# Four-layer network on one core: softmax reciprocals turned by DMA and set into PSUM by ScalarE, 5x5 convolutions that add to the shared sum in place, and a smaller pace

## The chip, the cores and the metric

The kernel runs on one core of one Trainium2 chip. The metric is the device time of one launch in microseconds (us). The engines of the core are TensorE (PE in the profile, its weight loads PEld), VectorE (DVE), ScalarE (ACT), GpSimd (POOL) and SyncE (SP), which here only issues DMAs. Each works through its own queue in order.

## The reference

Four images of 128 channels and 64 x 64 pixels pass through four residual layers. Each layer is `x = x + layer(groupnorm(x))` in float32.

```python
# layer 0: full attention over the 4096 pixels of an image, one head of 128
scores = einsum('bic,bjc->bij', q, k) * c ** -0.5
attn = softmax(scores, axis=-1)
out = einsum('bij,bjc->bic', attn, v)
# layer 1: a 5x5 convolution, its kernel built from radial weights
c = build_kernel(weightsxx, weightsidentity, XhatXhat, identity, indsxx, indsidentity)
x = conv(pad(x, 2), c)
# layer 2: two selective scans (one direction each), 64 channels, 64 states
dA = exp(delta[..., None] * A);  dBx = (delta * xt)[..., None] * Bm[:, :, None, :]
h = associative_scan(a1*a2, a2*b1 + b2)      # along the 4096 pixels
y = einsum('bldn,bln->bld', h, Cm) + D * xt
# layer 3: a 3x3 convolution (its offsets are zero) and a bias
```

## The kernel before

**Two streams of work.** The scans of layer 2 are cut into ticks: `scan_core` runs over 4 images x 4 chunks of 1024 pixels x 2 directions x 16 groups of states x 2 halves of channels, 1024 ticks in all, 256 to an image. A tick multiplies the drive on POOL (line 1268), takes the decay's exponential on ScalarE (1261), runs the recurrence on VectorE (`tensor_tensor_scan`, 1278), and multiplies by C on VectorE (1281) or, in a fixed share of the ticks, on POOL (1299). TensorE sums states into `y` (1317) every few ticks. Everything else (attention, convolutions, the scans' operands, the way back to the output) is a chain of Python generators, `images()`, whose `yield` values say how much TensorE work was just written.

**The order is written by hand.** `manual_schedule` leaves the order of instructions as the program writes it. Between the two halves of a tick the loop draws from `images()` until a credit is used up:

```python
PRODUCT, HOP, SLOT, PACE, ENDPACE, AHEAD = 0.86, 1.7, 0.7, 2.8, 1.5, 4
credit = min(credit + pace / 2, pace)
while credit > 0:
    credit -= next(work, pace)
```

So `PACE` sets how much of an image is written beside one tick; in the last image's scan it is `ENDPACE`. `before(b)` is called four ticks (`AHEAD`) before image b's scan begins: where that image's first operands are not written yet, it draws `images()` without a limit until they are. Image 0 has no scan beside it until its operands exist.

**Attention** goes over 8 blocks of 512 queries, each with 32 steps of 128 keys. Step u writes the scores of u (`sc`, line 487), their exponential on ScalarE into a ring of 8 slots in the tile `exchange` (493), and the product with the values of step u - 2 into the PSUM bank `acc` (499). The sums of the exponentials come in two ways. In image 0 (`fill` set) VectorE and POOL add every other step's tile into `sided` and `sidep` (541). In images 1 to 3, four matmuls of 32 columns, one in each group of 32 PSUM partitions, add four steps at a time into the bank `zp` (521). When a block is done (two steps into the next), ScalarE copies the sums (`zs`, 547) and `acc` (`raw`, 552) to SBUF. Then `turn` (564) takes the sums through TensorE into columns, `invert` (573, 575) takes reciprocals on VectorE, `widen_out` (479) spreads them over partitions through TensorE, and `settle` (587, 588) multiplies and adds on VectorE; these stand 1, 2, 4 and 5 steps after, and use the bank `z`, which the next block's `zp` uses too. `turn` and `widen_out` each count one `PRODUCT`.

**The 5x5 convolution** (`conv_pairs`) makes two output rows at a time and goes over 4 chunks of 1024 pixels. In images 1 to 3 (`lean`) a chunk has three sums of products (969): one that both rows share (`pq`, 10 products) and one for each row (`pe`, 15 each). ScalarE copies the shared sum to SBUF (`q`, 982), and one matmul with the identity (996) adds it to each row's bank. Image 0 goes another way (`wide`), with POOL adding `q` to the rows.

**Queues and buffers that matter.** All loads of the scan go out on SP: `br` and `cr` (1239), 512 KB each, once in two ticks, and `de` and `dx` (1233) at changes of chunk. The tiles tagged `w` in the pool `bg` have four buffers, `raw` and `zs` one, the scan's rows three.

Of the kernel before, what the change touches and what calls it, by code (L numbers as in the profile page):

```python
# [32 lines left out]
P = 128  # L33
# [12 lines left out]
PRODUCT, HOP, SLOT, PACE, ENDPACE, AHEAD = 0.86, 1.7, 0.7, 2.8, 1.5, 4  # L46
# [6 lines left out]
def conv_preact_kernel(  # L53
# [388 lines left out]
    def attention(b, xs, xn, v, st, safe, loads):  # L442
# [15 lines left out]
        def row_max(blk):  # L458
# [14 lines left out]
            mb[blk] = pools["bg"].tile([P, MM], F32, tag="w", bufs=4, name=f"mb_{b}_{blk}")  # L473
# [69 lines left out]
        def evict_sums(blk):  # L543
            zs = None
            if not fill:
                zs = pools["bg"].tile([P, MM], F32, tag="zs", bufs=1, name=f"zs_{b}_{blk}")
                nc.scalar.copy(zs, zp.pop(blk))
            state[blk] = None, zs

        def evict(blk):  # L550
            raw = pools["bg"].tile([P, MM], F32, tag="raw", bufs=1, name=f"raw_{b}_{blk}")
            nc.scalar.copy(raw, acc.pop(blk))  # L552
            state[blk] = raw, state[blk][1]
# [44 lines left out]
        for u in range(N):  # L598
# [11 lines left out]
            if w >= 0:  # L610
# [224 lines left out]
    def conv_pairs(b, xs, tag, st, st2, lean):  # L835
# [89 lines left out]
        steps, done = [], None  # L925
# [17 lines left out]
        for c in range(L // CH):  # L943
            j = c * CK
            if c < 2:
                piece(2 + c)
            if c < 3:
                differences(c + 1)
            accs = [
                (bank("s", f"pq_{b}_{c}"), ((SUM12, image, 2 * j + 2), (SUM34, image, 2 * j + 4))),  # L950
                (bank("a", f"pe0_{b}_{c}"),
                 ((0, image, 2 * j), (1, diff, j), (3, diff, j + 1))),
                (bank("z", f"pe1_{b}_{c}"),
                 ((0, image, 2 * j + 1), (2, diff, NP + j + 1), (4, diff, NP + j + 2))),
            ]
            if wide:
                total, first, last = (combo(n) for n in range(3))
                accs = [
                    (accs[0][0], (accs[0][1][1], (HSUM, total, j))),
                    (bank("y", f"pm_{b}_{c}"), ((HDIF, diff, j),)),  # L960
                    (accs[1][0], ((0, first, j), (3, diff, j + 1))),
                    (accs[2][0], ((2, last, j), (4, diff, NP + j + 2))),
                ]
            for n, (acc, parts) in enumerate(accs):
                k, total = 0, len(parts) * K5
                for w, view, r in parts:
                    for dx in range(K5):
                        k += 1
                        nc.tensor.matmul(  # L969
                            flat(acc), matrix(w, dx), view(r, dx),  # L970
                            start=k == 1, stop=k == total and (n == 0 or not lean),
                        )
                        if k == 3 and done is not None:
                            done()
                            done = None
                        if k % 3 == 0:
                            yield 3 * PRODUCT
                if n == 0:
                    qs = pools["bg"].tile([P, MM], F32, tag="w", bufs=4, name=f"q_{b}_{c}")

                    def done(acc=acc, qs=qs, c=c):
                        nc.scalar.copy(qs, acc)
                        for y in range(0 if lean else 2):
# [4 lines left out]
                elif wide and n == 1:  # L988
# [686 lines left out]
```

## Time and profile before

| | |
|---|---|
| median of 3 runs | 4425.56 us (4419.15 to 4431.18) |
| the profiled execution | 4426.94 us, of which the span is 4425.1 us |
| TensorE, VectorE, POOL, ScalarE busy | 88%, 84%, 81%, 54% of the span |
| image 0 alone, to the first tick's drive | 694.7 us |
| 1024 ticks, first to last drive | 694.7 to about 4361 us |
| DMA | 726 MB, mean 164 GB/s |

The profile cuts the span into 40 slices, each with the busy share of every engine in tenths. Groups of instructions carry the line, the engine, the tiles, the count, the busy time, the mean of one in nanoseconds, and the engine's idle time just before them with what ended it. A float32 product shows as two TensorE records[...]; the records overlap, and their ends are modelled, so distances between starts are used for TensorE.

### The profile page before, as it was taken

Reading aid. Unit: us, or ns where it says so; the run is one execution under the profiler, and the core shown is the slowest. Engines: PE = TensorE matmul, PEld = TensorE weight load, DVE = VectorE, ACT = ScalarE, POOL = GpSimd, SP = SyncE. Lnnn points to the kernel's source line nnn. Section 1 sums busy time; section 2 is a strip of 40 time slices with the busy share of each in tenths; the row PEclk is TensorE's granted clock in tenths of the full one; section 3 lists DMA queues with packets and bytes.
Section 4 is the critical chain, followed back from the end, with each engine's and each line's share of the span. In section 5 each row is a group of like instructions: output and inputs, shape, how many; then the busy total and the mean of one; then the engine's idle time right before and its main releaser. Section 6 shows DMA issues by size and latency. Waiting matters only on the chain. (4 is left out here: it accounts for less than half of the span.)

```text
span 4425.1 us, 42907 instructions
## 1 busy us (share of the span) xinstructions
PE 3896.3 (88%) x13352; PEld 1486.0 (34%) x13352; DVE 3702.6 (84%) x3471; ACT 2377.4 (54%) x4301; POOL 3603.6 (81%) x1713
## 2 busy tenths in 40 slices
PE   8999997999999979999989889999989657575667
PEld 4444433333333323333333333333333112121212
DVE  4722217999999989999999889999999899999996
ACT  3333217666665376666664576666643754444533
POOL 3433307999999968999989889999999789999995
PEclk9999999999999989999999989999999868787888
DMA  1000016545555565544545564555555666656562
GB/s 64 21 1 1 0 53 231 185 167 176 177 176 182 176 238 198 176 176 168 185 173 181 201 228 168 175 177 175 176 181 177 223 221 206 228 195 232 187 227 84
DMA packets 216302, 726.05 MB, mean 164 GB/s; under 512 B 26240, under 2 KB 27520, under 8 KB 215808
## 3 DMA queue, kind: packets, MB, share of 16 engines
q1 hardware_dynamic: 214144, 722.49, 47.1%
q8 instruction: 107, 1.75, 0.2%
q14 instruction: 131, 1.07, 0.1%
q10 hardware_dynamic: 1920, 0.73, 0.1%
HBM read 653.98 MB, written 69.14 MB: 163 GB/s over the span
## 5 line engine op out<-in xcount | busy, mean ns | idle before, releaser
L1268 POOL TENSOR_TENSOR db<-dx,br 128x1024 f32<-128x1024 f32 x1024 | 2399.5, 2366 | 224.8 <-DMA dx<-dxd 76.7
L1261 ACT ACTIVATE da<-de,a_neg 128x512 f32<-128x512 f32 (+1 forms) x1640 | 1303.1, 797 | 759.6 <-DVE da L1278 305.0
L487 PE MATMUL sc<-r,x 128*128 128x512 f32 x2048 | 1082.2, 611 | 22.5 <-ACT last L1294 9.7
L499 PE MATMUL acc<-exchange,v 128*128 128x512 f32 x2048 | 1048.6, 594 | 2.7 <-ACT raw L552 0.5
L1299 POOL TENSOR_TENSOR hc<-hc,cr 128x1024 f32<-128x1024 f32 x386 | 913.3, 2366 | 22.9 <-ACT last L1294 20.9
L1281 DVE TENSOR_TENSOR hc<-da,cr 128x512 f32<-128x512 f32 (+1 forms) x1003 | 839.5, 837 | 65.7 <-issue 1.3
L1278 DVE TENSOR_TENSOR_SCAN da<-da,last,db 128x512 f32<-128x512 f32 (+1 forms) x480 | 863.1, 1798 | 22.6 <-POOL db L1268 17.7
L493 ACT ACTIVATE exchange<-sc 128x512 f32<-128x512 f32 x1024 | 603.6, 589 | 503.1 <-PE sc L487 494.6
L1317 PE MATMUL y<-hc,sel 128*32 128x512 f32 x4096 | 604.8, 650 | 284.4 <-POOL hc L1299 230.9
L487 PEld LDWEIGHTS sc<-r,x 128*128 128x128 f32 x2048 | 361.8, 190 | 596.5 <-issue 376.7
L499 PEld LDWEIGHTS acc<-exchange,v 128*128 128x128 f32 x2048 | 386.9, 190 | 500.6 <-issue 478.5
L1278 DVE TENSOR_TENSOR_SCAN hc<-da,last,db 128x512 f32<-128x512 f32 (+1 forms) x288 | 490.9, 1705 | 6.4 <-ACT da L1261 3.3
L1278 DVE TENSOR_TENSOR_SCAN da<-da,da,db 128x512 f32<-128x512 f32 x365 | 469.7, 1287 | 6.8 <-ACT da L1261 6.6
L541 POOL TENSOR_TENSOR sidep<-sidep,exchange 128x512 f32<-128x512 f32 x120 | 170.8, 1423 | 273.4 <-ACT exchange L493 271.1
L1317 PEld LDWEIGHTS y<-hc,sel 128*32 128x32 f32 x4096 | 114.4, 113 | 715.5 <-POOL hc L1299 315.2
L1278 DVE TENSOR_TENSOR_SCAN hc<-da,hc,db 128x512 f32<-128x512 f32 x251 | 322.0, 1283 | 32.7 <-ACT da L1261 8.9
L541 DVE TENSOR_TENSOR sided<-sided,exchange 128x512 f32<-128x512 f32 x120 | 95.9, 799 | 221.7 <-ACT exchange L493 220.3
L1278 DVE TENSOR_TENSOR_SCAN da<-da,db 128x512 f32<-128x512 f32 (+1 forms) x158 | 232.4, 1471 | 13.1 <-ACT da L1261 10.1
L703 PE MATMUL pcm<-xpm,cs 128*128 128x512 f32 x432 | 214.5, 646 | 25.2 <-ACT xpm L392 25.2
L969 PE MATMUL pe<-df,exchange 128*128 128x512 f32 x480 | 214.2, 595 | 0.0
L521 PE MATMUL zp<-exchange,ones 128*32 128x512 f32 x1536 | 205.3, 601 | 9.6 <-DVE xs L588 9.5
L1294 ACT COPY last<-da 128x1 f32<-128x1 f32 x474 | 73.8, 156 | 259.7 <-DVE hc L1281 257.2
(239 smaller groups left out, 2838.8 us busy)
## 6 DMA issues: line engine op xcount, KB each, us to landing
br<-bm SPq DMA_DIRECT2D x512, 512.0 KB, 5.2
cr<-cm SPq DMA_DIRECT2D x512, 512.0 KB, 4.0
de<-dd SPq DMA_DIRECT2D x64, 512.0 KB, 4.9
dx<-dxd SPq DMA_DIRECT2D x64, 512.0 KB, 6.2
x<-in_x_dram SPq DMA_DIRECT2D x16, 512.0 KB, 6.0
xs<-in_x_dram SPq DMA_DIRECT2D x16, 512.0 KB, 6.6
xsd<-xs SPq DMA_DIRECT2D x16, 512.0 KB, 6.8
xcd<-xc SPq DMA_DIRECT2D x16, 512.0 KB, 2.9
```

The costliest lines, as they stand in the source:

```text
L487: nc.tensor.matmul(sc, xn[:, bass.ts(j, P)], rq[blk], start=True, stop=True)
L493: nc.scalar.activation(pt, sc, AF.Exp)
L499: nc.tensor.matmul(acc[blk], v[:, j, :], ring[:, u % NRING, :], start=j == 0, stop=j == NJT - 1)
L541: eng.tensor_tensor(s, s, ring[:, u % NRING, :], ALU.add)
L703: nc.tensor.matmul(acc.rearrange("p (r w) -> p r w", w=W), weights[:, t, :], xp[:, y : y + RPM, dx : dx + W], start=t == 0, stop=t == k * ...
L969: nc.tensor.matmul(flat(acc), matrix(w, dx), view(r, dx), start=k == 1, stop=k == total and (n == 0 or not lean),)
L1261: nc.scalar.activation(da, rep["de", b, c, d, g][:, bass.ts(h, size)], AF.Exp, scale=a_neg[:, at(i)])
L1268: nc.gpsimd.tensor_tensor(dbs[i], rep["dx", b, c, d, g], rows["b", b, c, d, q], ALU.mult)
L1278: nc.vector.tensor_tensor_scan(h, da, db[:, cut], before, ALU.mult, ALU.add)
L1281: nc.vector.tensor_tensor(hc[:, cut], h, rows["c", b, c, d, q][:, cut], ALU.mult)
L1299: nc.gpsimd.tensor_tensor(hcs[i], hcs[i], rows["c", b, c, d, q], ALU.mult)
L1317: nc.tensor.matmul(y[r : r + SG, :], sel, hcs[first + gg][:, bass.ts(h, MM)], start=False, stop=q == NQ - 1, tile_position=(0, r), skip_gr ...
```

## The change

*Attention.* `turn`, `invert` and `widen_out` stay only for the last block of an image. For the others, the block's sums, already in SBUF, are written to DRAM (`spill`), read back so that partition p holds the sums of queries 4p to 4p + 3 (`gather`), added and inverted on VectorE (`invert_rows`), written to DRAM (`put_rows`) and read back as one row to all partitions (`fetch_rows`). When the next block is done, ScalarE copies that tile into a PSUM bank (`stage_rows`), and `settle` follows a step later. In image 0 the two side tiles are first summed by two matmuls of 32 columns in `evict_sums`. `raw` moves to the `w` buffers, and `mb`, used only in a second pass for extreme inputs, takes its old one.

*Convolution, images 1 to 3.* ScalarE copies the shared sum of a chunk from its bank into the first row's bank; the first row's products are added there in place, and the second row's in the shared bank itself. The identity matmuls go. The order becomes: shared sum of chunk c, second row of chunk c - 1, first row of chunk c; the shared sums alternate between the banks `s` and `z`.

*Pace.* `PACE` goes from 2.8 to 2.75.

```diff
-PRODUCT, HOP, SLOT, PACE, ENDPACE, AHEAD = 0.86, 1.7, 0.7, 2.8, 1.5, 4
+PRODUCT, HOP, SLOT, PACE, ENDPACE, AHEAD = 0.86, 1.7, 0.7, 2.75, 1.5, 4
...
 def evict_sums(blk):
...
+            elif blk + 1 < NM:
+                zs = pools["bg"].tile([P, MM], F32, tag="zs", bufs=1, name=f"zs_{b}_{blk}")
+                pz = bank("z", f"pz_{b}_{blk}")
+                for g, e in enumerate("dp"):
+                    nc.tensor.matmul(
+                        pz[g * 32 : (g + 1) * 32, :], ones[:, :32], sides.pop((blk, e)),
+                        start=True, stop=True, tile_position=(0, g * 32), skip_group_check=True,
+                    )
+                nc.scalar.copy(zs[:64], pz[:64])
...
+        RUN = MM // P
+
+        def spill(blk):
+            raw, zs = state[blk]
+            n = 2 if fill else 4
+            zd = dram.tile([4, MM], F32, tag="zp", name=f"zd_{b}_{blk}")
+            nc.sync.dma_start(zd[:n], zs[0 : n * 32 : 32, :])
+            state[blk] = raw, zd[:n]
+
+        def gather(blk):
+            raw, zd = state[blk]
+            zt = small.tile([P, 4, RUN], F32, tag="zt", name=f"zt_{b}_{blk}")
+            n = zd.shape[0]
+            nc.sync.dma_start(zt[:, :n, :], zd.rearrange("g (p j) -> p g j", j=RUN))
+            state[blk] = raw, zt[:, :n, :]
+
+        def invert_rows(blk):
+            raw, zt = state[blk]
+            z = zall[:, b * NJT + blk * TPM : b * NJT + (blk + 1) * TPM]
+            nc.vector.tensor_reduce(z, zt.rearrange("p g j -> p j g"), AX.X, ALU.add)
+            zr = small.tile([P, RUN], F32, tag="zr", name=f"zr_{b}_{blk}")
+            nc.vector.reciprocal(zr, z)
+            state[blk] = raw, zr
+
+        def put_rows(blk):
+            raw, zr = state[blk]
+            zd = dram.tile([P, RUN], F32, tag="zd", name=f"zi_{b}_{blk}")
+            nc.sync.dma_start(zd, zr)
+            state[blk] = raw, zd
+
+        def fetch_rows(blk):
+            raw, zd = state[blk]
+            rb = pools["bg"].tile([P, MM], F32, tag="w", bufs=4, name=f"rb_{b}_{blk}")
+            row = zd.rearrange("p j -> (p j)").unsqueeze(0)
+            nc.sync.dma_start(rb, row.to_broadcast([P, MM]))
+            state[blk] = raw, rb
+
+        def stage_rows(blk, tag):
+            raw, rb = state[blk]
+            pb = bank(tag, f"rz_{b}_{blk}")
+            nc.scalar.copy(pb, rb)
+            state[blk] = raw, pb
...
                 if d == NJT - 1:
                     evict_sums(blk - 1)
                     evict(blk - 1)
-                    for n, f in ((1, turn), (2, invert), (4, widen_out), (5, settle)):
+                    for n, f in (
+                        (2, spill), (4, gather), (7, invert_rows), (9, put_rows), (11, fetch_rows)
+                    ):
                         after(u, n, f, blk - 1)
+                    if blk > 1:
+                        stage_rows(blk - 2, "z")
+                        after(u, 1, settle, blk - 2)
+                    cost += PRODUCT if fill else 0.0
             for f, args in later.pop(u, ()):
                 f(*args)
-                cost += PRODUCT if f in (turn, widen_out) else 0.0
...
         values(N - 4)
+        stage_rows(blk - 1, "s")
         yield PRODUCT
         while due:
             sums(due.pop(0)[0])
             yield PRODUCT
+        settle(blk - 1)
...
+        def shared_of(c):
+            j = c * CK
+            held[c] = bank("sz"[c % 2], f"pq_{b}_{c}")
+            yield from group(
+                held[c], ((SUM12, image, 2 * j + 2), (SUM34, image, 2 * j + 4))
+            )
+
+        def second_of(c):
+            nonlocal done
+            j, acc = c * CK, held.pop(c)
+            yield from group(
+                acc, ((0, image, 2 * j + 1), (2, diff, NP + j + 1), (4, diff, NP + j + 2)), True
+            )
+            done = lambda: add(c, 1, acc)
+
+        def first_of(c):
+            nonlocal done
+            j, acc = c * CK, owns.pop(c)
+            yield from group(
+                acc, ((0, image, 2 * j), (1, diff, j), (3, diff, j + 1)), True
+            )
+            done = lambda: add(c, 0, acc)
+
+        def part(c):
+            owns[c] = bank("a", f"pe0_{b}_{c}")
+            nc.scalar.copy(owns[c], held[c])
+
+        for c in range(NCK + 1 if lean else 0):
+            if c < NCK:
+                advance(c)
+                yield from shared_of(c)
+                done = lambda c=c: part(c)
+            if c > 0:
+                yield from second_of(c - 1)
+            else:
+                yield HOP
+                done()
+                done = None
+            if c < NCK:
+                yield from first_of(c)
...
-                    if lean:
-                        nc.tensor.matmul(acc, ident, qs, start=False, stop=True)
-                        yield PRODUCT
```

`group` writes the products of one sum (with its last argument true, without a fresh start of the bank), calls `done()` after the third product and yields three `PRODUCT` at a time; image 0's path goes through it too, unchanged in its products.

More of the change, by code (lines that the diff above doesn't have):

```diff
@@ L472, in row_max @@
             spread(pb, m)
-            mb[blk] = pools["bg"].tile([P, MM], F32, tag="w", bufs=4, name=f"mb_{b}_{blk}")
+            mb[blk] = pools["bg"].tile([P, MM], F32, tag="raw", bufs=1, name=f"mb_{b}_{blk}")
             nc.scalar.copy(mb[blk], pb)
@@ L550, in evict @@
+        def fetch_rows(blk):
[9 more added lines that the diff above has]
+            state[blk] = raw, pb
         def evict(blk):
-            raw = pools["bg"].tile([P, MM], F32, tag="raw", bufs=1, name=f"raw_{b}_{blk}")
+            raw = pools["bg"].tile([P, MM], F32, tag="w", bufs=4, name=f"raw_{b}_{blk}")
@@ L924, in conv_pairs @@
         K5 = 5
-        steps, done = [], None
+        done = None
         taps5 = more[0] if wide else exchange(b)[:, : NTAP * C].rearrange("p (k c) -> p k c", c=C)
@@ L941, in add, with advance @@
             st2.squares(i, chunk(xs, c, y), xs[:, 0:1])
-        for c in range(L // CH):
-            j = c * CK
+        def advance(c):
             if c < 2:
@@ L948, in conv_pairs @@
                 differences(c + 1)
-            accs = [
[L950 to L954, printed above, removed]
-            ]
[L956 to L963, printed above, removed]
@@ L964, in conv_pairs, with group @@
-            for n, (acc, parts) in enumerate(accs):
[L965 to L977, printed above, removed]
+        def group(acc, parts, begun=False):
+            nonlocal done
+            k, of_all = 0, len(parts) * K5
+            for w, view, r in parts:
+                for dx in range(K5):
+                    k += 1
+                    nc.tensor.matmul(
+                        flat(acc), matrix(w, dx), view(r, dx),
+                        start=k == 1 and not begun, stop=k == of_all, skip_group_check=lean,
+                    )
+                    if k == 3 and done is not None:
+                        done()
+                        done = None
+                    if k % 3 == 0:
+                        yield 3 * PRODUCT
@@ new lines, in conv_pairs @@
+        NCK, held, owns = L // CH, {}, {}
+        def shared_of(c):
[11 more added lines that the diff above has]
+            done = lambda: add(c, 1, acc)
@@ new lines, in first_of @@
+        def first_of(c):
+            nonlocal done
+            j, acc = c * CK, owns.pop(c)
+            yield from group(
+                acc, ((0, image, 2 * j), (1, diff, j), (3, diff, j + 1)), True
+            )
+            done = lambda: add(c, 0, acc)
[11 more added lines that the diff above has]
+                yield HOP
+                done()
+                done = None
+            if c < NCK:
+                yield from first_of(c)
@@ new lines, in conv_pairs @@
+        for c in range(0 if lean else NCK):
+            j = c * CK
+            advance(c)
+            total, first, last = (combo(n) for n in range(3))
+            accs = [
+                (bank("s", f"pq_{b}_{c}"), ((SUM34, image, 2 * j + 4), (HSUM, total, j))),
+                (bank("y", f"pm_{b}_{c}"), ((HDIF, diff, j),)),
+                (bank("a", f"pe0_{b}_{c}"), ((0, first, j), (3, diff, j + 1))),
+                (bank("z", f"pe1_{b}_{c}"), ((2, last, j), (4, diff, NP + j + 2))),
+            ]
+            for n, (acc, parts) in enumerate(accs):
+                yield from group(acc, parts)
@@ L982, in done @@
                         nc.scalar.copy(qs, acc)
-                        for y in range(0 if lean else 2):
+                        for y in range(2):
                             nc.gpsimd.tensor_tensor(
@@ L987, in conv_pairs @@
                     yield PRODUCT
-                elif wide and n == 1:
+                elif n == 1:
                     def done(acc=acc, c=c):
```

## The prediction

> **What bounds the kernel now.** I read the page's 40 slices first, then the windows by stage, VectorE's groups in one attention stage, who waits for whom, and TensorE's timeline at a block boundary.
>
> ```profile
> PE   8999997999999979999989889999989657575667
> DVE  4722217999999989999999889999999899999996
> ...
> 60.00:500.00 440.00, 438.16 (x1159) 203.95 (x1157) 174.29 (x211) 156.83 (x268) 165.60 (x122) 1.00 0.01 6
> 780.00:1372.00 592.00, 579.78 (x2249) 218.16 (x2248) 564.12 (x582) 384.72 (x792) 555.81 (x242) 1.00 0.52 179
> 1559.00:1593.00 34.00, 27.92 (x115) 9.14 (x115) 26.60 (x40) 25.86 (x42) 20.35 (x13) 0.83 0.65 238
> 1593.00:1658.00 65.00, 49.33 (x196) 21.15 (x196) 53.55 (x68) 54.34 (x90) 45.01 (x23) 0.90 0.70 240
> ```
>
> A window's row gives its length, then busy us (and count) of PE, PEld, DVE, ACT and POOL. Two regimes show. Until about 690 us image 0 has no scan beside it, and TensorE alone is full: 438 of 440 us from 60 to 500. From the first tick (694.7 us) to about 4360 the 1024 scan ticks run, and in an attention stage three engines are nearly full: TensorE 98%, VectorE 95%, POOL 94%. TensorE's share says least, since its ends are modelled. VectorE's groups decide:
>
> ```profile
> L1281 DVE TENSOR_TENSOR hc<-da,cr 128x512 f32<-128x512 f32 x205 | 141.9, 692 | 11.8
> L1278 DVE TENSOR_TENSOR_SCAN da<-da,da,db 128x512 f32<-128x512 f32 x102 | 131.2, 1286 | 0.1
> L1278 DVE TENSOR_TENSOR_SCAN da<-da,last,db 128x512 f32<-128x512 f32 x77 | 98.2, 1275 | 4.6 <-POOL db L1268 4.3 <-ACT exchange L493 0.4
> L1278 DVE TENSOR_TENSOR_SCAN hc<-da,hc,db 128x512 f32<-128x512 f32 x68 | 87.3, 1283 | 9.1 <-ACT da L1261 2.7
> L1278 DVE TENSOR_TENSOR_SCAN da<-da,db 128x512 f32<-128x512 f32 x25 | 30.3, 1214 | 0.0
> ```
>
> VectorE idles 28 us of these 592 (171 ticks of 3.46 us), and only 7.9 us has a releaser; the rest is gaps mostly under 0.3 us between a scan and what reads it. Second sign: the first 64 ticks start their scans from zero (1214 ns instead of 1275 to 1286, two to a tick), and ticks 16 to 64 take 3.37 us where 64 to 128 take 3.475. Scans 0.12 us shorter, ticks 0.10 shorter: the tick follows VectorE. TensorE is close behind, not in front. At the hand-over to the next image (1559 to 1658) VectorE idles 19 us of 99.
>
> **What the Trainium skill says.** "DMA: Bandwidth & Descriptors", Latency and other measured facts, puts a DMA's fixed cost near 2 us, more under load. Here even 0.2 KB loads (skip) took 4.2 us to land, 256 KB row writes 3.3 to 4.1, so I count 4 to 5 us for each new DMA. The same page, Rules for kernel authors: a DMA that reads what another wrote must wait for its completion semaphore, so each block's four DMAs form a chain of two round trips on SP; and DMA doesn't reach PSUM, which is why a ScalarE copy is needed. "PSUM — Partial Sum Buffer", Specifications, calls ScalarE faster to PSUM than to SBUF; the trace agrees weakly (tanh 661 ns to PSUM, 687 to SBUF), so I price the copies at the 585 ns of zs. "TensorE: Matmul & The Clock Gate", Part 3: matmuls in different column groups run together; the trace agrees, below.
>
> **Part by part.**
>
> ```profile
> 205.07 1.11 PE L499 MATMUL acc<-exchange,v 128*128 128x512 f32 x2
> ...
> 207.71 1.11 PE L487 MATMUL sc<-r,x 128*128 128x512 f32 x2
> ...
> 212.94 1.05 PE L479 MATMUL pzb<-ident,zr 128*128 128x128 f32 x8
> ...
> 1001.79 1.07 PE L521 MATMUL zp<-exchange,ones 128*32 128x512 f32 x8
> ```
>
> *Image 0.* A product is two records (two passes), 0.86 us from start to start. Between the acc at 205.07 and the sc at 207.71 lie 2.64 us; without the turn it would be 0.86, so it costs 1.78. The widening at 212.94 costs 0.89, as acc (212.09) to sc (213.84) is 1.75 there. Together 2.67 us a block. The new pz is two matmuls of 32 columns in two column groups: four of these (zp) take about 1.0 us, so two take 0.86 to 1.0. Saved 1.65 us on each of seven blocks (the last keeps the old way): 11.5. The new pz stands in the step of the last side sum, not one later; at the second boundary VectorE is behind (that sum ends 157.4 us, TensorE is ready 156.3), which gives 1.1 back. **-10.4 us**, all on the path, as TensorE is full.
>
> *Images 1 to 3, TensorE.* A block loses eight short matmul records each of turn (0.81 us: 813.31 to 814.12) and widening (0.9): 1.7 us, by eight blocks but the last, 12 us; the convolution loses eight identity products of 0.86, 6.9 us. 19 us an image, 57 in all, beside VectorE's scans. It counts only where VectorE waits for TensorE through ScalarE's queue, where the exponentials of sc and of the decays stand in line. The attention windows' VectorE waits with a releaser are 7.9, 10.2 and 12.4 us; I take a sixth: **-5 us** (bounds 0 and -30).
>
> *The pacing.* In units of the credit (one product 0.86) an image costs: attention 515.1, convolution 148.7, the rest 52.3, sum 716.2; at 2.8 to a tick, 255.8 of its 256 ticks. After: attention less 7 x 2 x 0.86 = 12.0; convolution less twelve yields of 0.86 plus one HOP of 1.7, 8.6; sum 695.5, at 2.75, 252.9 ticks. Before, the operands of images 1, 2 and 3 are short at the hand-over by 5.6, 0.7 and 1.4 units, issued in one go with no tick between; after, they stand 1, 3 and 6 ticks ahead. A unit is about 1 us of TensorE: 7.7 us of bursts go, and first loads that came late (dx 4.6 us at 1593 to 1658, dx 3.2 and de 1.8 at 3476 to 3537) come sooner. VectorE's idle there, 19, 16 and 18 us, is the ceiling, much of it the exp-log chain, which stays. **-10 us** (0 to -25).
>
> *Ticks that change stage.* The last stage begins 11 ticks sooner. Its ticks use whole 1024-element scans (2.34 + 2/3 x 1.225 = 3.16 us of VectorE) against 3.30 in attention (564 over 171); only about 5 ticks change form, as convolution ticks already have the wide one: **-1 us**.
>
> *What is added.* Per block 4 SP DMAs (224 in all), one ScalarE copy of 0.585 us (in the convolution the PSUM copy takes the place of q at the same price), on VectorE a tensor_reduce and a reciprocal where a copy of 0.15 and the same reciprocal were: nothing. ScalarE is at 65%: its copies hide, unless decays come late; +1. The wait to fear is invert_rows, which stands in VectorE's queue before the scans and waits for gather. SP's own queue first:
>
> ```profile
> SPq L1239 <- POOL hc L1299: 279.8, 66, 9.7
> SPq L1239 <- DVE hc L1281: 144.8, 48, 6.2
> ```
>
> SP stands most of the time before a cr load until its buffer is free; in the trace that load goes out 0.2 to 0.5 us before VectorE starts the tick it was written before (90% within 2.7 us either way). So SP is in step with VectorE. Gather goes out right behind such a load; invert_rows comes three steps later, 3 x 1.94 / 2.75 = 2.1 ticks or 7.3 us. Landing of 5 us, its 16-byte pieces and the cr before it included, leaves about 2. Loads behind the chain (br, cr) may be held up to 4 us by a landing; br goes out some 10.7 us before POOL's product needs it and lands in 5.2, so that is covered. Settling a block later frees z earlier than before. **+3 us** for now and then a late gather (0 to +60).
>
> Sum: -10.4 - 5 - 10 - 1 + 1 + 3 = -22. The profiled execution took 4426.9 (span 4425.1), 1.4 over the median of the runs, 4425.56. So 4426.9 - 22 = 4405, less 1.4: **4403 us**.
>
> **Rivals.** *TensorE was the bound of attention too.* For it: 98% busy. Against: the zero-start ticks. It would give the ceilings: 30 us from attention and 20 at the hand-overs instead of 15, so about 4370. *Only image 0 gains*: work that ends sooner merely waits, VectorE being full; 4425.6 - 10.4 and little else, 4414: no change that counts. For it: VectorE at 95%. Against: the bursts, which hold ticks up whatever the engine. *Late gather, slower*: if it lands late in most of the 21 blocks with scans beside them, VectorE stops each time. At 3 us each 63 us are added to the 4400 there would be without it: 4463. It decides from 1.2 us a block (26 us); over 1.8 it is slower beyond doubt. For it: one SP queue, with cr waits up to 9.7 us; against: SP's step with VectorE. *Or it isn't lighter*: 2.9% less work at 1.8% less pace is still a denser image; VectorE's side work gathers in fewer ticks. That is inside the range.
>
> **How the numbers follow.** Forecast 0.5 (4391 to 4412 by itself), TensorE-bound 0.22, only image 0 0.18, late gather 0.10. A measurement of this kernel tells 0.3%, 13 us, from no change: faster is under 4412. Forecast and TensorE rival lie almost wholly there, with a little of the third: 0.74; same 0.17; slower 0.09. The range takes the first three and a small late gather: 4372 to 4424.
>
> **What would show it.** First tick near 684 us, not 694.7. Attention ticks still near 3.46 us and VectorE at 95% or more. Less VectorE idle at the three hand-overs. No wait above 1 us at invert_rows, and zt landing in 5 us or less. A tick under 3.4 us in attention means TensorE was the bound; VectorE waits on zt adding to over 25 us, or POOL waits on br, mean the forecast failed.

## The result and the profile after

The changed kernel takes **4416.94 us**, median of 20 runs (4410.16 to 4424.51), against 4425.75 (20 runs, 4417.32 to 4431.18) for the kernel before: a ratio of 0.9983, 95% interval 0.9977 to 0.9990. That is 8.8 us less where 22 were forecast: the direction was right, the size less than half of it. The profiled execution took 4421.17 us (span 4419.4), 4.2 above its own median, so that the two profiles differ by 5.8 us only (4426.94 and 4421.17), and terms that come from single profiles are good to some 5 us.

From the page of the changed kernel, the same two rows of slices, and from its windows by stage the stretches that answer to those shown of before (length, then busy us and count of PE, PEld, DVE, ACT, POOL, then granted clock, DMA share and GB/s):

```profile
PE   8999998999998979999989889999989567574766
DVE  4722218999998989999989999999989899999996
...
60.00:500.00 440.00, 431.39 (x1024) 186.50 (x1022) 176.97 (x226) 165.56 (x287) 169.02 (x127) 0.99 0.04 11
780.00:1360.00 580.00, 563.24 (x2094) 201.78 (x2087) 555.36 (x574) 382.61 (x787) 548.34 (x239) 1.00 0.55 181
1549.00:1583.00 34.00, 31.92 (x119) 11.07 (x120) 27.85 (x32) 28.11 (x47) 23.80 (x12) 0.88 0.74 269
1583.00:1648.00 65.00, 43.73 (x190) 17.14 (x188) 58.31 (x69) 51.99 (x84) 51.36 (x27) 0.90 0.68 234
```

Image 0 still fills TensorE, with fewer products. The attention stage is what it was: VectorE 95.8% busy (555.36 of 580; 95.3% before), TensorE 97%. In the hand-over (the last two rows) VectorE now idles 12.8 us of 99, where it was 19.

VectorE's groups in the attention stretch of the changed kernel (count, busy us, mean ns, idle before them):

```profile
L1378 DVE TENSOR_TENSOR hc<-da,cr 128x512 f32<-128x512 f32 x202 | 139.6, 691 | 13.0 <-PE sc L487 0.4 <-issue 0.4
L1375 DVE TENSOR_TENSOR_SCAN da<-da,da,db 128x512 f32<-128x512 f32 x101 | 129.9, 1286 | 1.0 <-ACT da L1358 1.0
L1375 DVE TENSOR_TENSOR_SCAN da<-da,last,db 128x512 f32<-128x512 f32 x76 | 96.9, 1275 | 1.4 <-POOL db L1365 0.8 <-ACT exchange L493 0.3 <-ACT last L1391 0.2
L1375 DVE TENSOR_TENSOR_SCAN hc<-da,hc,db 128x512 f32<-128x512 f32 x67 | 86.0, 1283 | 8.2 <-ACT da L1358 1.5
```

The scans last what they did, and the tick in this stage stays at 3.45 to 3.50 us. So the work taken from TensorE did not shorten the tick in this stage.

The turn by DMA is in time. The new tile `zt`, images 1 to 3, with who kept its engine idle:

```profile
L572 SPq DMA_DIRECT2D zt<-zd x21: 371/386/593, 814.5 to 3152.4; - x21
L578 DVE TENSOR_REDUCE zall<-zt x21: 150/171/175, 821.9 to 3157.9; 128x4 f32<-128x16 f32 x21
its engine sat idle before it (us, times) until:
```

Under "sat idle before it" the answer lists no one: VectorE never waited for a gather.

**Image 0.** TensorE and ScalarE at the third block boundary of image 0 (start, length; the brackets give idle time before it):

```profile
203.43 1.02 PE L499 MATMUL acc<-exchange,v 128*128 128x512 f32 x2
...
204.38 0.62 PE L552 MATMUL pz<-sided,ones 128*32 128x512 f32 x1
204.39 0.62 PE L552 MATMUL pz<-sidep,ones 128*32 128x512 f32 x1
...
205.37 1.13 PE L487 MATMUL sc<-r,x 128*128 128x512 f32 x2
205.51 0.58 ACT L556 COPY zs<-pz 64x512 f32<-64x512 f32 x1 [1.22 <-PE pz L552]
205.99 0.58 ACT L604 COPY raw<-acc 128x512 f32<-128x512 f32 x1
...
206.62 1.12 PE L499 MATMUL acc<-exchange,v 128*128 128x512 f32 x2
```

The two products of 32 columns run side by side, as forecast. What was not foreseen is the step after: ScalarE copies `zs` first and `raw` behind it, and the next block's first `acc` needs the bank that `raw` empties: from `sc` at 205.37 to `acc` at 206.62 are 1.25 us, not 0.86. The attention of image 0 (first to last `sc`) went from 462.7 to 454.4 us, -8.3 where -10.4 was forecast, and the first tick's drive came 7.6 us sooner. It stands at 676.2 us on the clock of these windows, before at 683.8; the 694.7 given with the profile before counts from the trace's first record, some 11 us ahead, where 687.4 answers to it and 684 was forecast.

**A stall at the end of each attention stage.** The timeline of the changed kernel, image 2, last block:

```profile
2279.80 0.57 ACT L599 COPY rz<-rb 128x512 f32<-128x512 f32 x1
...
2283.07 0.75 DVE L640 SCALAR_TENSOR_TENSOR xs<-rz,bv_c,xs 128x512 f32<-128x512 f32 x1
...
2283.86 0.72 ACT L336 ACTIVATE junk<-xs,aw_e 128x512 bf16<-128x512 f32 x1 [2.08 <-DVE xs L640]
...
2284.58 0.56 ACT L547 COPY zs<-zp 128x512 f32<-128x512 f32 x1
...
2285.20 1.87 PE L616 MATMUL pz<-zsel,zs 128*128 128x1 f32 x8 [5.28 <-ACT zs L547]
...
2293.84 0.70 DVE L639 TENSOR_TENSOR pzb<-raw,pzb 128x512 f32<-128x512 f32 x1 [5.77 <-PE pzb L479]
```

In the tail, `settle` of block 6 is written ahead of `zs` of block 7. Its square sum (`junk`, line 336, on ScalarE) waits for VectorE, and `zs`, though its sums have been ready since 2278.9 (a modelled end), waits behind it in ScalarE's queue. TensorE stands idle 5.28 us, then runs at half its clock (granted 0.51 from 2285 to 2291), and VectorE waits 5.77 us for the last `pzb`. Image 1 shows 4.80 on TensorE and 4.16 on VectorE; image 3 loses 1.70. In the kernel before, image 2's `zs` starts right when its sums are done, and VectorE waits 1.20 us.

### The profile page after: what moved, and what is told of

Its sections match the earlier page's. It is cut to its first block, busy times and chain, and to the rows that moved or that the text cites. A ratio compares the mean times of both kernels' runs of the same rounds, so it can differ in the third digit from the quotient of the medians.

```text
span 4419.4 us, 42088 instructions
## 1 busy us (share of the span) xinstructions
PE 3847.5 (87%) x12828; PEld 1422.2 (32%) x12828; DVE 3696.7 (84%) x3456; ACT 2389.9 (54%) x4331; POOL 3612.0 (82%) x1717
## 5 line engine op out<-in xcount | busy, mean ns | idle before, releaser
L1414 PE MATMUL y<-hc,sel 128*32 128x512 f32 x4096 | 614.3, 654 | 309.5 <-POOL hc L1396 254.9
L1375 DVE TENSOR_TENSOR_SCAN da<-da,last,db 128x512 f32<-128x512 f32 (+1 forms) x474 | 852.0, 1797 | 31.7 <-POOL db L1365 21.8
L541 DVE TENSOR_TENSOR sided<-sided,exchange 128x512 f32<-128x512 f32 x120 | 97.5, 813 | 234.4 <-ACT exchange L493 233.4
L1014 PE MATMUL pq<-xpe,cs 128*128 128x512 f32 x280 | 135.0, 633 | 39.8 <-ACT xpe L392 39.8
```

The lines of the kernel that those rows point to most:

```text
L541: eng.tensor_tensor(s, s, ring[:, u % NRING, :], ALU.add)
L1375: nc.vector.tensor_tensor_scan(h, da, db[:, cut], before, ALU.mult, ALU.add)
L1414: nc.tensor.matmul(y[r : r + SG, :], sel, hcs[first + gg][:, bass.ts(h, MM)], start=False, stop=q == NQ - 1, tile_position=(0, r), skip_gr ...
```

## The experiments

In all of them the median is compared with runs of the kernel before on the same chip. These medians lie between 4423.8 and 4427.0 us, so that differences of 3 us between experiments from different chips say little.

### The stall in the tail

The changed kernel, with `settle` of the last block but one moved behind `turn`:

```diff
             yield PRODUCT
-        settle(blk - 1)
         for n in range(NRING - 4):
...
         turn(blk)
+        settle(blk - 1)
         values(N - 2)
```

> The changed kernel with one line moved: in the tail of attention the settle of block 6 is written after the turn of block 7 instead of before the copy of its sums. Theory (tail): in the changed kernel ScalarE's square of that settle stands in front of the copy zs and waits for VectorE, so zs came 5 us after its sums were done, TensorE idled 5 us before pz in images 1 to 3, VectorE 4.2, 5.8 and 1.7 us before the last settle, and the convolution began late. Expected: those idles go to about 1 us each, VectorE's idle in the three convolution stages falls from 52.6 to about 40 us, and the time is 10 to 15 us under the changed kernel: about 4404 us, ratio to the kernel before 0.995. Rival (the in-place convolution itself makes VectorE idle): the time stays within 3 us of 4417, ratio 0.998. Rival (late gather): no change either.

Measured: **4412.31** (0.9967, 0.9955 to 0.9979), 4.6 less than the change as it was made (5.9 when each is taken against the kernel before on its own chip), where 10 to 15 were expected. The windows show the place. Each line sums the stretches of one kernel over images 1 to 3 (length, then busy us of each engine); length less DVE is VectorE's idle time. The convolution in the kernel before:

```profile
sum 560.10, PE 530.20 PEld 209.99 DVE 520.15 ACT 225.85 POOL 520.76; mean PE 176.73 PEld 70.00 DVE 173.38 ACT 75.28 POOL 173.59
```

in the changed kernel:

```profile
sum 554.10, PE 515.78 PEld 206.64 DVE 501.45 ACT 224.47 POOL 501.15; mean PE 171.93 PEld 68.88 DVE 167.15 ACT 74.82 POOL 167.05
```

and with the late settle:

```profile
sum 547.30, PE 510.19 PEld 201.63 DVE 502.80 ACT 222.41 POOL 501.48; mean PE 170.06 PEld 67.21 DVE 167.60 ACT 74.14 POOL 167.16
```

40.0, 52.6 and 44.5 us of idle time (the stage begins in the tail of attention, so the stall falls into it). The late settle takes back 8.1 of the 12.7 that the change had added there; in the medians 4.6 to 5.9 of that shows.

### The two halves of the change, and the pace

The kernel before with the pace of the changed one, nothing else:

```diff
-PRODUCT, HOP, SLOT, PACE, ENDPACE, AHEAD = 0.86, 1.7, 0.7, 2.8, 1.5, 4
+PRODUCT, HOP, SLOT, PACE, ENDPACE, AHEAD = 0.86, 1.7, 0.7, 2.75, 1.5, 4
```

> The kernel before with PACE 2.75 alone. An image's 716.2 units then need 260.4 ticks of 256, so the bursts at the three hand-overs grow from 5.6, 0.7 and 1.4 units to about 12 each, 28 units more. Theory (VectorE sets the ticks; a burst stops them): 15 to 30 us slower, about 4445, ratio 1.005. Rival (a burst costs nothing because VectorE's own operand work runs in it): within 5 us of 4426, ratio 1.000.

Measured: 4452.69 (1.0051, 1.0038 to 1.0065). By the program's own count, work issued in one go at the hand-overs grows from 5.6, 0.7 and 1.4 units to 18.2, 11.9 and 12.6, and VectorE's idle time there from 53.5 to 82.7 us. With 35 more units in bursts the kernel is 26 us slower by the medians of 5 and 14 runs (17 to 29 by the interval): the bursts are real, and cost some 0.75 us a unit.

The kernel before with the new convolution alone, at pace 2.8 (attention as before):

```diff
+        def part(c):
+            owns[c] = bank("a", f"pe0_{b}_{c}")
+            nc.scalar.copy(owns[c], held[c])
...
-                    if lean:
-                        nc.tensor.matmul(acc, ident, qs, start=False, stop=True)
-                        yield PRODUCT
```

> The kernel before with the in-place convolution alone, PACE 2.8, attention as before. 8.6 units less to an image: bursts of images 1 to 3 go. Theory (tail): the convolution is harmless or helps, as TensorE has 21 us less and the bursts of 7.7 units go: 0 to 8 us faster, about 4421, ratio 0.999. Rival (the in-place convolution makes VectorE idle 12 us): 5 to 12 us slower than 4426, about 4434, ratio 1.002.

Measured: **4409.4** (0.9961, 0.9948 to 0.9975), -17.6: more than either theory gave it. By the program's count no work is left over at the hand-overs, and the three convolutions take 150 ticks instead of 159, the hand-overs 54 instead of 56. The 11 ticks so freed run in the last stage, at 3.25 us, where a convolution tick takes 3.52 and a hand-over tick about 5.7. In the traces VectorE's idle time over all ticks falls from 234.4 to 222.3 us and its busy time from 3430.0 to 3418.9. Of the 11 us of busy time 5.5 are nothing that the convolution does: twelve additions at the hand-overs took 15.7 us instead of 21.2, as 4 of them met a running GpSimd product instead of 8 (the last section has the cause).

The new attention alone, old convolution, pace 2.8:

```diff
-                    for n, f in ((1, turn), (2, invert), (4, widen_out), (5, settle)):
+                    for n, f in (
+                        (2, spill), (4, gather), (7, invert_rows), (9, put_rows), (11, fetch_rows)
+                    ):
```

> The changed attention alone, the convolution as before, PACE 2.8. Image 0 gains 8 us, attention's idle of VectorE falls a few us, the tail loses about 10. Theory (tail): 0 to 8 us faster than the kernel before, about 4421, ratio 0.999, with the same idle before the last settle (about 4 us an image) and TensorE idle of about 5 us before pz. Rival (convolution at fault): the whole gain of attention shows, 15 us and more, about 4409, ratio 0.996.

Measured: 4416.88 (0.9981, 0.9971 to 0.9991), -10.1, between the two expectations. Image 0 alone is worth about 8 of it, so that beside the old convolution the new attention of images 1 to 3 costs nothing that shows, the bursts that go with it included.

Both together at pace 2.8, that is the changed kernel with only the pace undone:

```diff
-PRODUCT, HOP, SLOT, PACE, ENDPACE, AHEAD = 0.86, 1.7, 0.7, 2.75, 1.5, 4
+PRODUCT, HOP, SLOT, PACE, ENDPACE, AHEAD = 0.86, 1.7, 0.7, 2.8, 1.5, 4
```

> The changed kernel with PACE 2.8 alone put back, the settle where the change has it. Theory (tail, pace harmless): 2 to 3 us under the changed kernel, about 4414, ratio 0.9975. Rival (the smaller pace lost the gain): about 4402, ratio 0.9945.

Measured: 4420.09 (0.9987, 0.9980 to 0.9993); neither expectation was met. The halves bring 10.1 and 17.6, and together at the same pace about 6. **They do not add.** Each frees the hand-overs of their bursts, which can be gained once only; that is a reason for some of it, and not shown to be all.

The late settle at pace 2.8:

```diff
-PRODUCT, HOP, SLOT, PACE, ENDPACE, AHEAD = 0.86, 1.7, 0.7, 2.75, 1.5, 4
+PRODUCT, HOP, SLOT, PACE, ENDPACE, AHEAD = 0.86, 1.7, 0.7, 2.8, 1.5, 4
...
-        settle(blk - 1)
...
         turn(blk)
+        settle(blk - 1)
```

> The changed kernel with the settle of block 6 moved behind the turn of block 7, and PACE back at 2.8: an image takes 248.4 ticks, image 3 is done at tick 750 and not 762. Theory (with VectorE the limit, only VectorE's work and the stops of its queue count; a smaller pace keeps more ticks in the stages where scans are cut in two, 3.30 us of VectorE against 3.16): 12 ticks by about 0.2 us less, about 4409, ratio 0.996. Rival (the smaller pace was what lost the gain, as it takes the room that the lighter image gave): about 4398, ratio 0.9935, near the sum of the two parts alone (-17.6 and -10.1).

Measured: 4418.49 (0.9984, 0.9976 to 0.9991), 6 slower than at 2.75; neither expectation was met. So by the medians the smaller pace is worth 3 to 6 us to the changed kernel (the intervals overlap), where it costs the old one 26. And at pace 2.8 the late settle brings 1.6 us only (4420.09 to 4418.49, on one chip): there VectorE waited for the last `pzb` 1.0 us in all three images even with the early settle, and not 11.6. How much the stall costs depends on the ticks that the tail falls beside.

### Which part of the new attention pays

The new attention in image 0 only; images 1 to 3 turn their sums on TensorE as before; new convolution, late settle, pace 2.8:

```diff
+                    for n, f in (
+                        (2, spill), (4, gather), (7, invert_rows), (9, put_rows), (11, fetch_rows)
+                    ) if fill else ((1, turn), (2, invert), (4, widen_out), (5, settle)):
                         after(u, n, f, blk - 1)
-                    if blk > 1:
+                    if fill and blk > 1:
                         stage_rows(blk - 2, "z")
                         after(u, 1, settle, blk - 2)
```

> The new attention in image 0 alone (with the late settle in its tail), images 1 to 3 attend as before; the in-place convolution; PACE 2.8. No DMA chain, no extra ScalarE copy and no extra settle beside the scans. Theory (in images 1 to 3 the DMA route gives VectorE nothing: the parts that pay are image 0's TensorE and the convolution): -17.6 of the convolution alone and about -8 of image 0, about 4401, ratio 0.994, the fastest so far. Rival (the route pays in images 1 to 3 too, and its gain is lost only in the tail): about 4408 to 4415, not under the changed kernel with the late settle (4412).

Measured: **4401.4** (0.9945, 0.9931 to 0.9959), which beats both kernels: 15.5 us faster than the changed one, 25 than the one before. It is the convolution's gain plus 8.0 for image 0. Beside the new convolution, the new attention in images 1 to 3 is a loss: 17 us at this pace with the late settle (4418.49), 11 at pace 2.75 (4412.31).

Why, is asked with kernels in which the scan ticks stand beside the same work. In the first, the changed kernel with late settle at pace 2.8 still charges two products for each block in images 1 to 3, though it no longer issues them:

```diff
                 f(*args)
+                cost += PRODUCT if not fill and f in (spill, gather) else 0.0
```

> The whole change with the late settle and PACE 2.8, but every block of images 1 to 3 still counts the two PRODUCT that turn and widening counted. Its ticks fall where those of the kernel with the new attention in image 0 alone fall (operands of image 3 done at tick 762), and TensorE simply has 1.7 us less in each of 21 blocks. Theory (denser images cost: with the charge gone the same credit holds more score and value products, and their exponentials, beside each tick): the loss against 4401 goes, 4397 to 4404, ratio 0.9945. Rival (the chain itself costs: DMAs, copies, waits): it stays 8 to 17 us slower than 4401, about 4413, ratio 0.997.

Measured: 4411.3 (0.9969, 0.9957 to 0.9981): 10 slower than the version above, whose stages begin at the same ticks, although TensorE has some 36 us less to do. So DMAs, copies and the later settle together cost 10 us more than the lighter TensorE brings. The trace shows where: the scans' waits for the exponential of the decay (`da`) are 43.9 us, 53 times, against 35.5, 43 times, in the version above. Without the charge (4418.49, above) it is 7 slower still; there the blocks also fall beside other ticks, so that this step can't be put down to density alone.

One suspected cost by itself: the version of 4401.4 with one more ScalarE copy per block in images 1 to 3, of `raw` into a bank that nothing reads (21 copies, 12 us of ScalarE):

```diff
+                    if not fill:
+                        nc.scalar.copy(bank("z", f"rz_{b}_{blk - 1}"), state[blk - 1][0])
```

> The kernel with the new attention in image 0 alone, plus one more ScalarE copy of 128x512 (0.59 us, SBUF to a PSUM bank, not used) after each block of images 1 to 3, where the staging copy would stand. It prices ScalarE's part: 21 copies, 12 us of ScalarE. Theory (ScalarE has room): within 3 us of 4401, ratio 0.9945. Rival (the row of copies delays the decays): 6 to 12 us slower, ratio 0.9965.

Measured: 4412.76 (0.9972, 0.9961 to 0.9983), **11 us for 12 us of copies** on an engine that is busy 65% of the attention stage. The three attention stretches of the version without the copy, summed:

```profile
sum 1918.70, PE 1887.18 PEld 706.75 DVE 1825.03 ACT 1250.19 POOL 1807.26; mean PE 629.06 PEld 235.58 DVE 608.34 ACT 416.73 POOL 602.42
```

and with it:

```profile
sum 1932.40, PE 1889.21 PEld 706.98 DVE 1826.04 ACT 1263.39 POOL 1807.56; mean PE 629.74 PEld 235.66 DVE 608.68 ACT 421.13 POOL 602.52
```

ScalarE works 13 us longer, VectorE as long as before, and VectorE's idle time (length less DVE) goes from 93.7 to 106.4 us. What the scans waited for over all ticks (us, times), without the copy:

```profile
  ACT da L1361: 35.5, 43
  POOL db L1368: 24.7, 26
```

and with it:

```profile
  ACT da L1363: 48.1, 56
  POOL db L1370: 29.0, 27
```

The scans wait for the exponential of the decay: 12.6 us more, as many as the copies take. `turn` had to wait for the copy's bank too (TensorE 4.9 us, 15 times), which may be part of it, and the profiled execution was 4.3 us above its own median.

**In the changed kernel itself this is not what the trace shows.** Its scans waited, over all ticks, for

```profile
  POOL db L1365: 33.7, 29
  ACT da L1358: 30.9, 37
```

and with the late settle for

```profile
  POOL db L1365: 34.5, 32
  ACT da L1358: 27.7, 31
```

They wait no longer for the decays than in the version of 4401.4 (35.5 us) or in the kernel before (33.9, and 25.0 for `db`, POOL's drive). What grew is the wait for the drive. VectorE's idle time from the first scan to the last is 225.7 us in the version of 4401.4, 237.5 in the changed kernel and 228.5 with the late settle: of the 11.8 us more, 9.0 go with the late settle. Besides, VectorE is busy 5.7 us longer with the late settle than in the version of 4401.4. Attention's own operations account for 0.4 us of that. The rest stands in twelve additions at the hand-overs, first in the version of 4401.4, then with the late settle (count, busy us, mean ns, idle before them):

```profile
L1217 DVE TENSOR_TENSOR exchange<-exchange,u 128x512 f32<-128x512 f32 x12 | 16.0, 1386 | 1.1 <-ACT u L1241 1.1
L1214 DVE TENSOR_TENSOR exchange<-exchange,u 128x512 f32<-128x512 f32 x12 | 22.6, 1940 | 0.7 <-ACT u L1238 0.7
```

So the row of copies is shown to cost where blocks fall beside the ticks of the version of 4401.4; in the changed kernel they fall beside others, and its loss shows in the tail, in waits for the drive and in these additions.

The other cost by itself: the same version, with the chain of four DMAs per block in images 1 to 3, whose result nothing uses:

```diff
+                    if not fill:
+                        for n, k in ((2, 0), (4, 1), (9, 2), (11, 3)):
+                            after(u, n, idle_chain, blk - 1, k, state[blk - 1][1])
```

> The kernel with the new attention in image 0 alone, plus the four DMAs of the chain in images 1 to 3 at the change's steps (2, 4, 9, 11), with nothing that waits for them. It prices the DMA chain on SP alone: 84 DMAs. Theory (SP's holds are covered, as spreading them changed nothing): within 3 us of 4401, ratio 0.9945, though POOL's waits for br may rise from 14 to 25 us. Rival (the DMAs on SP cost): 6 to 12 us slower, ratio 0.9965.

Measured: 4405.97 (0.9955, 0.9941 to 0.9968). 4.6 slower, with intervals that overlap, and in the profiled execution the ticks take 0.4 us longer: inconclusive, at most a few us.

### Could the order be mended?

Settle three steps later behind the copy in images 1 to 3, with the late settle of the tail; VectorE then no longer meets a fresh `rz`:

```diff
-                        after(u, 1, settle, blk - 2)
+                        after(u, 1 if fill else 4, settle, blk - 2)
```

> The changed kernel with the late settle in the tail, and in images 1 to 3 the settle of every other block four steps after its staging copy instead of one. Theory (VectorE's waits for rz, up to 2 us each, come from ScalarE's row of three copies zs, raw and rz; with four steps they are gone): 2 to 6 us under the kernel with the late settle alone, about 4408, ratio 0.996. Rival (these waits only move to the next scan): 4412, ratio 0.9967.

Measured: 4416.82 (0.9976, 0.9968 to 0.9983). The wait at `rz` was 1.5 us in the kernel with the late settle and is gone, but the time is 4.5 longer: neither expectation was met.

The chain spread, so that each DMA is issued when the one before has long landed:

```diff
-                        (2, spill), (4, gather), (7, invert_rows), (9, put_rows), (11, fetch_rows)
+                        (4, spill), (9, gather), (15, invert_rows), (18, put_rows), (23, fetch_rows)
```

> The changed kernel with the late settle in the tail, and the DMA chain of every block spread out: spill, gather, invert_rows, put_rows and fetch_rows 4, 9, 15, 18 and 23 steps after the block instead of 2, 4, 7, 9 and 11. Same work, same DMAs. Theory (the chain costs because SP, which works in order, stands before gather and fetch until the DMA they depend on has landed, so that br goes out late and POOL waits for it): SP's waits before gather and fetch, 48 us where they were looked at, go to under 10, POOL's waits for br fall from 24 to 34 us in the kernels with the chain to about 16, and the time is 3 to 8 us under the kernel with the late settle (4412), about 4407, ratio 0.9955. Rival (the extra ScalarE copies and the denser products are what costs): POOL's waits for br may fall, the time stays within 2 us of 4412 or rises, ratio 0.9967 or more.

Measured: 4413.36 (0.9974, 0.9966 to 0.9982), against 4412.31 without it. These are SP's waits for its own chain in the changed kernel:

```profile
SPq L572 <- DMA zd<-zs: 28.1, 11, 5.2
SPq L593 <- DMA zi<-zr: 24.2, 10, 3.7
```

Spread, the two fall from 52 us to 2, but POOL's waits for `br` do not fall (26.8 us; 24.1 with the late settle alone), and the time doesn't move: SP's standing in line was not on the path.

### Which engine is the limit

Three kernels add load to the kernel before, in images 1 to 3. First the short matmuls of `turn` and `widen_out` three times, +82 us of TensorE:

```diff
-            for t in range(TPM):
+            for t in [t for t in range(TPM) for _ in range(3 if b > 0 else 1)]:
...
-            spread(pb, zr)
+            for _ in range(3 if b > 0 else 1):
+                spread(pb, zr)
```

> The kernel before, with each short matmul of turn and of widen_out written three times in images 1 to 3 (the same values again): about 3.4 us more TensorE work in each of 24 blocks, 82 us in all, no other engine's work changed. Theory (VectorE sets the attention ticks, TensorE has some 5% to spare): most of it hides, 0 to 25 us slower, about 4438, ratio 1.003. Rival (TensorE sets them): all of it shows, 60 to 82 us, about 4500, ratio 1.017.

Measured: 4494.87 (1.0146, 1.0130 to 1.0162), +69. But 44 of the 66 us of VectorE's new idle time stand right at `zall` and at the settle, which wait for these very matmuls: the test priced mostly a latency, and not the load.

So the load was put where nobody waits for it, on every eighth score product, issued twice (+82 us):

```diff
-                nc.tensor.matmul(sc, xn[:, bass.ts(j, P)], rq[blk], start=True, stop=True)
+            for _ in range(2 if b > 0 and u % 8 == 4 else 1):
+                nc.tensor.matmul(sc, xn[:, bass.ts(j, P)], rq[blk], start=True, stop=True)
```

> The kernel before with every eighth score product of images 1 to 3 written twice (the same values): 96 products of 0.86 us, 82 us of TensorE, spread evenly and not in front of anything that VectorE itself waits for. Theory (VectorE sets attention, TensorE has little but some to spare): well under half shows, 0 to 35 us slower, about 4445, ratio 1.004, and no wait of VectorE for a TensorE result grows. Rival (both are at the limit, an added TensorE us costs nearly a us, as when turn and widening were tripled): 55 to 82 us slower, about 4495, ratio 1.016.

Measured: 4469.93 (1.0102, 1.0087 to 1.0118), +43, between the two expectations: half of it shows. It reaches VectorE through ScalarE's queue: from 720 to 3420 us the scans' waits for the decays go from 30.8 to 72.8 us, behind exponentials of `sc` that wait for TensorE.

And five in-place maxima on `raw` ahead of each settle, load for VectorE:

```diff
+            for _ in range(5 if b > 0 else 0):
+                nc.vector.tensor_tensor(raw, raw, raw, ALU.max)
             nc.vector.tensor_tensor(pb, raw, pb, ALU.mult)
```

> The kernel before, with five more VectorE operations of 128x512 (max of raw with itself, 0.69 us each) ahead of each settle of images 1 to 3: 3.45 us in each of 24 blocks, 83 us of VectorE in all. Theory (VectorE sets the ticks): nearly all of it shows, 65 to 85 us slower, about 4505, ratio 1.018. Rival (TensorE sets them): it hides in VectorE's gaps, 0 to 25 us, about 4438.

Measured: 4587.72 (1.0359, 1.0345 to 1.0374), +162. The maxima held VectorE for 141 us and not 83 (the last section says why), and all of it shows, with some more. VectorE sets the tick, as far as a load in one place shows. For TensorE one load was tried: some 40 us of slack in three attention stages that then runs out would give +43, and so would a price of half a us for each us of load. What relief of TensorE is worth these loads don't show, and the kernels with less TensorE work have the added copies and DMAs too.

## Why the prediction was right and wrong

- **Image 0, -10.4.** Right, and nearly in size: -8.3 in the trace, 8.0 between two kernels on the chip. The step missed ScalarE's order `zs`, `raw`, which holds the next `acc`.
- **TensorE relief in attention, -5.** It can't be seen in the time. VectorE's idle time in the three attention stages went from 100.7 to 93.7 us, as if the forecast held; but the fastest version, whose attention in these images is that of before, has 93.7 too. The path was right: the scans' waits for the decays over all ticks fell from 33.9 to 30.9 us, and to 22.4 with the new attention alone. But those for POOL's drive rose from 25.0 to 33.7 and 34.9. The reasoning from the zero-start scans held (VectorE's load shows in full), and the sixth taken on top of it had no ground.
- **Pacing and hand-overs, -10, and ticks that change stage, -1.** The mechanism was right: the bursts are gone, the last stage begins 11 ticks sooner, and VectorE's idle time at the hand-overs falls from 53.5 to 48.0 us. The size was off, and low: the convolution alone brings 17.6, some 5 of them by luck, going by the traces (the twelve additions). The second term was mis-sized because it counted only the width of a scan. It should have compared whole ticks, 3.52 in convolution and over 5 at a hand-over with 3.25 in the last stage.
- **What is added: "ScalarE is at 65%: its copies hide ...; +1".** This is the step that failed. With the +3 for late gathers, the new attention's own cost was put at 4 us; against the kernel that keeps the old attention in images 1 to 3 it costs 15.5, of which 10 remain at the same ticks with the late settle. The reason given fails by itself: 21 copies at that place, on an engine with a third of its time free, cost 11 us. At a block's end `zs`, `raw` and `rz` stand in a row in ScalarE's queue, some 1.5 us from the first start to the next instruction, and what stands behind them waits. In the changed kernel, though, the decays' waits did not grow, so that this row is shown for other ticks only. Here 9.0 us of VectorE's idle time are the tail's. The copy was priced with the Trainium skill in mind ("PSUM — Partial Sum Buffer", Specifications: ScalarE is faster to PSUM than to SBUF), at the 585 ns of `zs`; `rz` took 610, so that no such gain shows for this copy, whose source is another too. The 224 new DMAs of the prediction are 112 (four for each of 28 blocks); its sum doesn't rest on that.
- **"Settling a block later frees z earlier than before."** So it does, but that sentence looked at the bank and not at ScalarE's queue. In the tail the square sum of a settle written ahead of `zs` held TensorE and VectorE: 4.6 to 5.9 us in the medians, 8.1 to 9.0 us of VectorE's idle time in the profiles.
- **Late gather, +3 and a rival.** Priced too high: no wait for `zt` at all. Loads behind the chain were held more than thought harmless, though: POOL's waits for `br` over all ticks went from 15.6 to 34.2 us, which the prediction had named as a sign of being wrong.
- **"Less work at less pace is still a denser image"**, put inside the range: taking the charge away at pace 2.8 costs 7 us by the medians, and the smaller pace gives 3 to 6 back.

The rival "only image 0 gains" came closest (4414), by luck: the convolution's gain was there, and the attention of images 1 to 3 ate it. The steps -17.6 (convolution), -8.0 (image 0) and +15.5 (attention of images 1 to 3, with its tail) are differences of successive medians, so that their sum has to agree with the -8.8 measured; it is no test. So the rival had the number and not the reason: not one term that stayed at zero, but two that cancel. The TensorE rival fell with the tick at 3.45 to 3.50.

Open stays how the loss divides. Of the 15.5, the version that still charges shows 10 from copies, DMAs and the later settle, less what the lighter TensorE brings (copies by themselves 11, with a caveat; DMAs by themselves about 5, within error); the late settle in the tail is worth some 5 at pace 2.75. At the changed kernel's own ticks no run takes the copies or the DMAs away by themselves, so that what they cost there is not shown.

## What to carry to other kernels

Price an instruction added to an in-order engine by what stands behind it at that place, and not by the engine's share: if its products feed the engine that sets the pace, a copy can cost its full time, as 21 did here. Then look for the same wait in the trace of the change itself: here it was another. When an operation is moved, follow each instruction that it issues on every queue, the small reductions at its end included. Where several parts relieve the same wait, count that gain once, and try each part alone: here one part carried the gain, and another took it back. And ask of a longer busy time whether it is work: an operation that waits for another engine after its start counts as busy.

## What the runs showed of the hardware

- Where TensorE had been idle 5.28 us, its granted clock was 0.51 in the next 6 us, and a pair of products took 2.05 us instead of about 1.1: the stall goes on costing after it is over. The Trainium skill says so ("TensorE: Matmul & The Clock Gate", Part 1: half the clock after an idle window of about 3.4 us), and the trace agrees.
- Of the 120 maxima of 128x512 that have one tile of SBUF as both inputs and output, 85 took about 0.69 us and 35 between 1.1 and 4.9, most about 2.7; together 141 us. The trace shows what makes it one or the other: none of the 85 began while a GpSimd product was under way, all of the 35 did, and 33 of them ended 0.55 us after that product (two after the next). The additions in place at the hand-overs show the same (0.68 us, or to 0.55 us after the product). The scans' products with C, which read one input from PSUM, took 0.68 to 0.69 us in the kernel before, though 659 of 730 began beside a running GpSimd product.
- A ScalarE copy of 128x512 from SBUF into PSUM took 610 ns (`rz`, median of 21), and 590 where it was the unused one; from PSUM to SBUF it took 585 (`zs`).
